# Attention's first steps beside the last feed-forward batch: another order, and key products copied out of PSUM

## The chip, the cores and the metric

The kernel runs on one core of one Trainium2 chip. The metric is the device time of one execution in microseconds; of several runs the median is taken. The core's engines are TensorE (PE, matrix products; its weight loads are shown as PEld), VectorE (DVE), ScalarE (ACT) and GpSimd (POOL), each with its own queue of instructions, and SyncE (SP), which here only issues DMA transfers. All data is float32.

## The reference

One "macaron" layer on x of shape (4, 512, 512): half a feed-forward block, an attention with a gated delta rule, and half a feed-forward block again, each behind a layer norm and added to its input.

```python
x = x + 0.5 * ffn(layernorm(x), gate_cp, up_cp, down_cp)
x = x + attn(layernorm(x), W_qkvz, W_ba, conv_w, dt_bias, A_log, norm_w, W_out)
x = x + 0.5 * ffn(layernorm(x), gate_cp, up_cp, down_cp)

# ffn: the three 2048 x 512 weights are cubic splines through control points
inter = silu(h @ gate_w.T) * (h @ up_w.T)
return inter @ down_w.T

# attn: 16 key heads, 32 value heads, 128 wide
q, k, v, z = split(x @ W_qkvz);  b_gate, a_gate = split(x @ W_ba)
q, k, v = silu(causal_conv4(q, k, v))
q, k = rms_norm(q) / 128, rms_norm(k) / 128**0.5
beta = sigmoid(b_gate);  g = -exp(A_log) * softplus(a_gate + dt_bias)
for t in range(512):                    # per batch and value head
    S = S * exp(g[t])
    S = S + outer(k[t], (v[t] - k[t] @ S) * beta[t])
    o[t] = q[t] @ S
return (silu(z) * rms_norm(o) * norm_w) @ W_out
```

The kernel does the recurrence in chunks of 128 tokens. In a chunk a lower triangular matrix of key products, weighted by decay and beta, has to be inverted; its 32 x 32 diagonal blocks are inverted first, for four heads at once.

## The kernel before, in words

**Three parts.** `ffn` is called for the first block, `attention` is a generator of steps, and `ffn` is called again. The first `ffn` is handed attention's generator as `beside`: while its last batch runs, each of its own steps is followed by one `next` on the generator (function `run`), and after the last of them the generator is run until it yields `None`. What is left is run after `ffn` has returned.

**The last feed-forward batch.** In the passage at hand `run` is called three times: with what is left of batch 2 (16 steps, together with the 16 gathers of batch 3's hidden rows, which POOL issues as indirect DMAs at L458), with batch 3's own steps (first four returns of batch 2: transposes at L509 and the additions on DVE at L537; then 32 steps of L482, L492, L495 and L498), and with batch 3's four returns. The hidden rows are stored by SP at L449, and a gather needs all of them.

**Order.** PE, DVE, ACT and POOL run this passage in the order in which the program emits it. SP is not in that hand-written order: a planner places its DMA issues. A calendar (`later`) puts follow-up work a number of ticks behind a step: a projection's taps one tick later, its tanh three after that, its silu one more.

**Attention's first steps** (`begin`, L1632 to the `yield None`). For batch 0: load constants; load four tiles of 128 rows of `x1` (two buffers, so tiles 2 and 3 follow tiles 0 and 1); statistics, one power on POOL and one normalisation for each tile (L920 to L927); four transposes `turn_x` (L934); the gate products `raw` (L941) with `gates_of` and `log1p`; then eight keys, one in seven ticks. `sums` (L1001 to L1016) makes the decays and stores them to DRAM. A key is: its weights loaded (L1080, one buffer), a projection in four steps (L1030), taps on ACT and DVE (L1038, L1040), tanh and silu (L1048, L1052), products of the key with itself in 32-wide blocks (`blocks`, L1061, into the tile `pkk`), their diagonal sums (L1066 to L1069), a power on POOL (L1071), weights (L1109 to L1119), and `below`: a scan over the decay row `ad` (L1126) and the product `dd` of `pkk` with its result (L1129). `invert` (L1140 to L1159) works on the `dd` of four keys; here two of its steps are put behind each tick.

**Banks.** Until the feed-forward block has given its PSUM back, attention has two banks, each with one buffer: `bank` hands out "kk" for `pkk`, and "bank" for all others (transposes, gate products, sums, projections). The banks of the main loop (`at_pa` and others) are opened when these two are closed.

**The main loop** takes one head in each of 66 slots (64 heads of four batches), each with its queries, values, gates, recurrence, output and, eight heads ahead, another key. In that loop keys have buffers of their own (`pa` is not `None`).

Of the kernel before, what the change touches and what calls it, by code (L numbers as in the profile page):

```python
# [11 lines left out]
F32 = mybir.dt.float32  # L12
BF16 = mybir.dt.bfloat16
AF = mybir.ActivationFunctionType
ALU = mybir.AluOpType
# [249 lines left out]
def tile_macaron(ctx, tc, x, w_qkvz, w_ba, conv_w, dt_bias, a_log, norm_w, w_out, cps, consts, grid, starts, out):  # L265
# [33 lines left out]
    def ffn(src, dst, build, beside=iter(())):  # L299
        with ExitStack() as st:  # L300
# [339 lines left out]
            with by_hand():  # L640
                also = beside if B > 2 else iter(())
                run(*left, also)
                run(*turn_of(B - 1), also)
                run(plan["tail"], [], also)
                drain()
                for step in beside:
                    if step is None:
                        break
# [167 lines left out]
    def attention():  # L816


        with ExitStack() as st:
# [14 lines left out]
            sm = pool("at_sm", 2)  # L834
            sn = pool("at_sn", LEAD + 3)
            w1 = split("at_w1", 1, "za", "ge", "w_k", "dd", "inv", "inv_tmp", "rn", "rt")
            w2 = split("at_w2", 2, "sq", "xnT", "acc", "th", "ad", "wed")
            wkeys = pool("at_k", LEAD + 2)
            first_banks = ExitStack()
            pf = first_banks.enter_context(tc.tile_pool(name="at_pf", bufs=1, space=PSUM))  # L840
# [2 lines left out]
            def bank(p, name, shape):  # L843
                if p is None:
                    return pf.tile(shape, F32, name=name, tag="kk" if name == "pkk" else "bank")
                return p.tile(shape, F32, name=name, tag="bank")


            cst = ac.tile([P, C_ID], F32, name="cst")
            nc.sync.dma_start(cst, consts[:, :C_ID])  # L850
            ones = ac.tile([P, P], F32, name="ones")
            nc.vector.memset(ones, 1.0)
            gt = cst[:, C_GT : C_GT + P]
            le = cst[:, C_LE : C_LE + P]
            idb = cst[:, C_IDB : C_IDB + BLK]

            cw = ac.tile([P, 4 * NK, 4], F32, name="cw")
            nc.sync.dma_start(cw, conv_w.rearrange("(n p) k -> p n k", p=P))
            nc.vector.tensor_scalar(cw, cw, 0.5, None, ALU.mult)
            wba = ac.tile([P, NC, 4 * NK], F32, name="wba")  # L860
            nc.sync.dma_start(wba, w_ba.rearrange("(c p) n -> p c n", p=P))
            dtb = ac.tile([P, NG], F32, name="dtb")
            nc.sync.dma_start(dtb, dt_bias.partition_broadcast(P))
            nega = ac.tile([P, NG], F32, name="nega")
            nc.sync.dma_start(nega, a_log.partition_broadcast(P))
            nc.scalar.activation(nega, nega, AF.Exp)
            nc.vector.tensor_scalar(nega, nega, -1.0, None, ALU.mult)
            nwh = ac.tile([P, 1], F32, name="nwh")
            nc.sync.dma_start(nwh, norm_w.rearrange("(p o) -> p o", o=1))
            nc.vector.tensor_scalar(nwh, nwh, 0.5, None, ALU.mult)  # L870

# [24 lines left out]

            tts = [ac.tile([P, 8, P], F32, name=f"tt{k}", tag=f"tt{k}") for k in range(2)]
            nn = ac.tile([64, 8, 64], F32, name="nn")  # L900
            for x_ in (*tts, nn):
                nc.vector.memset(x_, 0.0)

            decay_c, decay_b = (
                [dram.tile([NK, NT, 2, P], F32, name=f"decay_{k}{b}", tag=f"decay_{k}{b}") for b in range(B)] for k in "cb"
# [2 lines left out]
            def begin(b):  # L908


                bt, box = {}, {}

                def load(t):
                    xt = w2.tile([P, H], F32, name="xt", tag="sq")
# [141 lines left out]
            def products(out, v):  # L1056

                for t in range(NT):
                    for o in range(0, P, BLK):
                        blk = v[:, t * P + o : t * P + o + BLK]  # L1060
                        nc.tensor.matmul(out[o : o + BLK, t, :], blk, blk, start=True, stop=True)  # L1061
# [12 lines left out]
            def keys(b, n, bt, s, dd, slot):  # L1074

                at = n * 6 * DK + DK

                def load():
                    s["w_k"] = w1.tile([P, NC, DK], F32, name="w_k")
                    nc.sync.dma_start(s["w_k"], w_qkvz[:, at : at + DK].rearrange("(c p) k -> p c k", p=P))  # L1080

                def dest():
                    s["k"] = wkeys.tile([P, S], F32, name="k")
                    return s["k"]

                dense = project(lambda: s["w_k"], 0, NK + n, dest, bt)

                def decay():
                    s["ad"] = w2.tile([P, NT, 2, BLK], F32, name="ad")
                    for o in range(0, P, BLK):  # L1090
                        src = decay_b[b][n].rearrange("t r q -> (t r) q")[:, o : o + BLK]
                        nc.sync.dma_start(
                            s["ad"][o : o + BLK].rearrange("p t r q -> p (t r) q"), src.partition_broadcast(BLK)
                        )

                def blocks():
                    pkk = bank(pa, "pkk", [P, NT, BLK])
                    s["pkk"] = pkk
                    products(pkk, s["k"])

                    def squares():
                        ms, rs = mean_square(pkk, "k")
                        later(3, lambda: weights(ms, rs))

                    later(1, squares)

                def weights(ms, rs):
                    irk = sn.tile([P, NT], F32, name="irk")
                    nc.vector.scalar_tensor_tensor(irk, ms, DK**0.5, rs, ALU.mult, ALU.mult)  # L1109
# [12 lines left out]

                def below():
                    wed = s["wed"]
                    flat = wed.rearrange("p t r q -> p (t r q)")
                    nc.vector.tensor_tensor_scan(  # L1126
                        flat, s["ad"].rearrange("p t r q -> p (t r q)"), flat, 0.0, ALU.mult, ALU.add
                    )
                    nc.vector.tensor_tensor(  # L1129
                        dd()[:, 8 * slot : 8 * slot + 8, :].rearrange("p (t r) q -> p t r q", r=2),  # L1130
                        bc(s["pkk"], 2, 2), s["wed"], ALU.mult,
                    )

                return dict(load=load, dense=dense, decay=decay, blocks=blocks)
# [494 lines left out]
                    due()  # L1629
                    yield True  # L1630

            batches[0], load, turn_x, raw, sums = begin(0)  # L1632
            load(0)
            load(1)
            yield from ticks(9)
            turn_x(0)
            load(2)
            yield from ticks(2)
            turn_x(1)
            load(3)  # L1640
            yield from ticks(8)
            turn_x(2)
            yield from ticks(2)
            turn_x(3)
            yield from ticks(1)
            raw()
            yield from ticks(1)
            ahead = min(LEAD, N)
            made, first = [], None
            for un in range(ahead + 2):  # L1650

                if un < ahead:
                    made.append(keys_of(un))
                    made[un]["load"]()
                if un >= 2:
                    made[un - 2]["blocks"]()
                for i in range(7):
                    if un < ahead and i < NC:
                        made[un]["dense"][i]()
                    if un == 1 and i == 4:  # L1660
                        sums()
                    if 1 <= un <= ahead and i == 5:
                        made[un - 1]["decay"]()
                    yield from ticks(1)
                    for _ in range(2):
                        next(first or iter(()), None)
                if un == GRP + 1:
                    first = invert(diag[0], inverse[0])
            drain()
            for _ in first:  # L1670
                pass
            yield None
            first_banks.close()
            for f in backs:
# [49 lines left out]
```

## Time and profile before

| | us |
|---|---|
| median of 3 runs | 3895.45 (3895.11 to 3900.36) |
| the profiled execution | 3850.33 |
| its span, first to last instruction | 3848.6 |
| PE busy in it | 3584.5 (93%) |
| DVE busy | 2633.1 (68%) |
| ACT busy | 1461.8 (38%) |
| POOL busy | 851.7 (22%) |
| passage: last batch's leftovers begin on PE | 341.2 |
| first transpose of attention | 361.5 |
| first key's projection begins | 394.5 |
| last return of the feed-forward block on PE | 449.5 |
| first query projection of the main loop begins | 519.65 |
| first query products (`pqq`, L1061) begin | 530.56 |

A busy share is a mean over stages with different limits, so it says little of a passage of 180 us. Read the passage by stretches: which engine is idle, and which event ended its wait. An engine name with a q behind it (SPq) is that engine's queue. In lines of time the columns are start, duration, engine, source line, operation, tiles written and read, how many instructions were merged, and in brackets the idle time before with what ended it. In lines of waits they are the sum, the number and the longest.

### The profile page before, as it was taken

Reading aid. Unit: us, or ns where it says so; the run is one execution under the profiler, and the core shown is the slowest. Engines: PE = TensorE matmul, PEld = TensorE weight load, DVE = VectorE, ACT = ScalarE, POOL = GpSimd, SP = SyncE. Lnnn points to the kernel's source line nnn. Section 1 sums busy time; section 2 is a strip of 40 time slices with the busy share of each in tenths; the row PEclk is TensorE's granted clock in tenths of the full one; section 3 lists DMA queues with packets and bytes.
Section 4 is the critical chain, followed back from the end, with each engine's and each line's share of the span. In section 5 each row is a group of like instructions: output and inputs, shape, how many; then the busy total and the mean of one; then the engine's idle time right before and its main releaser. Section 6 shows DMA issues by size and latency. Waiting matters only on the chain.

```text
span 3848.6 us, 62481 instructions
## 1 busy us (share of the span) xinstructions
PE 3584.5 (93%) x24568; PEld 1970.3 (51%) x24568; DVE 2633.1 (68%) x5931; ACT 1461.8 (38%) x3432; POOL 851.7 (22%) x658
## 2 busy tenths in 40 slices
PE   5997768999999999999999999999999999997998
PEld 2332335555555555555555555555555555553333
DVE  5232577877888888787788887887888777652321
ACT  2221124444444444444444444444444444442221
POOL 2113112212222222122222221222222222120221
PEclk8999889999999999999999999999999999997999
DMA  4435311122212222122122221221122211112452
GB/s 142 154 131 177 102 46 50 58 66 63 59 59 59 61 86 76 43 66 72 60 58 86 61 69 55 61 61 58 58 81 68 67 50 56 50 36 97 152 200 91
DMA packets 303093, 302.25 MB, mean 79 GB/s; under 512 B 96880, under 2 KB 231312, under 8 KB 302224
## 3 DMA queue, kind: packets, MB, share of 16 engines
q1 hardware_dynamic: 292560, 264.70, 22.0%
q0 software_dynamic: 10240, 33.56, 2.8%
q8 instruction: 194, 3.18, 0.3%
q14 instruction: 99, 0.81, 0.1%
HBM read 247.60 MB, written 50.59 MB: 77 GB/s over the span
## 4 chain that ended last, share of the span: by engine, by line
PE 43%; DVE 36%; ACT 8%; POOL 6%; issue 3%; DMA 3%; SPq 1%; DVEq 0%; POOLq 0%; ACTq 0%
DVE acc L1040 13%; PE py L1492 7%; PE pz L1344 6%; DVE vT L1052 4%; PE pj L1030 4%; PE y L492 3%; POOL oo L1465 3%; DVE ee L1212 3%; PE pg L439 3%; PE pu L439 3%; PE pks L1383 2%; POOL orr L1464 2%; ACT tq L1400 2%; PE pu L1329 2%; ACT th L1048 2%
## 5 line engine op out<-in xcount | busy, mean ns | idle before, releaser
L1040 DVE SCALAR_TENSOR_TENSOR acc<-pj,cw,acc 128x511 f32<-128x511 f32 (+2 forms) x768 | 573.7, 747 | 166.1 <-ACT acc L1038 148.0
L1030 PE MATMUL pj<-xnT,w_v 128*128 128x512 f32 x1024 | 519.4, 600 | 0.0
L1492 PE MATMUL py<-w_o,gT 128*128 128x512 f32 x1024 | 514.9, 616 | 0.4
L1344 PE MATMUL pz<-w_z,xnT 128*128 128x512 f32 x1024 | 514.1, 613 | 0.0
L448 DVE TENSOR_TENSOR ffn_it<-pu,ffn_sg 128x512 f32<-128x512 f32 x128 | 88.4, 691 | 365.8 <-PE pu L439 252.5
L1030 PE MATMUL pj<-xnT,w_q 128*128 128x512 f32 x512 | 255.8, 603 | 4.9 <-DVE dd L1129 4.9
L1030 PE MATMUL pj<-xnT,w_k 128*128 128x512 f32 x512 | 260.1, 612 | 0.0
L1038 ACT ACTIVATE acc<-pj,cw 128x512 f32<-128x512 f32 x256 | 175.1, 684 | 212.9 <-PE pj L1030 212.0
L1400 ACT ACTIVATE tq<-pks,rqe 128x128 f32<-128x128 f32 x384 | 120.0, 364 | 340.0 <-DVE rq L1241 204.9
L1048 ACT ACTIVATE th<-acc 128x512 f32<-128x512 f32 x256 | 163.0, 637 | 214.9 <-DVE acc L1040 213.2
L1470 ACT ACTIVATE oo<-oo,orr 128x128 f32<-128x128 f32 x512 | 162.6, 389 | 204.4 <-POOL oo L1465 204.4
L1492 PEld LDWEIGHTS py<-w_o,gT 128*128 128x128 f32 x1024 | 171.5, 192 | 106.2 <-issue 95.2
L1344 PEld LDWEIGHTS pz<-w_z,xnT 128*128 128x128 f32 x1024 | 169.9, 191 | 99.4 <-issue 88.4
L1071 POOL TENSOR_TENSOR rsq<-msq,phalf 128x4 f32<-128x4 f32 x64 | 64.8, 1013 | 684.9 <-DVE msq L1069 684.9
L1071 POOL TENSOR_TENSOR rsk<-msk,phalf 128x4 f32<-128x4 f32 x64 | 65.9, 1029 | 658.9 <-DVE msk L1069 649.2
L1030 PEld LDWEIGHTS pj<-xnT,w_v 128*128 128x128 f32 x1024 | 170.2, 191 | 70.1 <-issue 63.5
L1226 POOL TENSOR_TENSOR ks<-kn,ws 128x1024 f32<-128x1024 f32 x64 | 121.6, 1901 | 375.7 <-DVE ws L1219 352.3
L1052 DVE SCALAR_TENSOR_TENSOR vT<-th,acc 128x512 f32<-128x512 f32 x128 | 185.1, 1446 | 22.8 <-ACT th L1048 22.8
L458 POOL DMA_INDIRECT nat<-hid,idx x128 | 122.2, 955 | 305.1 <-PE y_pt L509 104.2
L1458 DVE TENSOR_REDUCE om<-osq 128x4 f32<-128x512 f32 x128 | 87.1, 681 | 138.8 <-ACT osq L1457 138.8
L1151 DVE TENSOR_TENSOR inv<-inv,inv_tmp 128x30 f32<-128x30 f32 (+14 forms) x480 | 168.4, 351 | 16.5
L1408 PEld LDWEIGHTS pzz<-rr,tt 128*128 128x128 f32 x768 | 114.6, 192 | 113.0 <-issue 54.7
(205 smaller groups left out, 6868.3 us busy)
## 6 DMA issues: line engine op xcount, KB each, us to landing
hid<-ffn_it SPq DMA_DIRECT2D x128, 256.0 KB, 2.0
w_v<-in_L_attn_W_qkvz SPq DMA_DIRECT2D x64, 512.0 KB, 3.6
w_z<-in_L_attn_W_qkvz SPq DMA_DIRECT2D x64, 512.0 KB, 5.1
ab<-decay_c SPq DMA_DIRECT2D x64, 512.0 KB, 3.7
w_o<-in_L_attn_W_out SPq DMA_DIRECT2D x32, 1024.0 KB, 5.5
w_k<-in_L_attn_W_qkvz SPq DMA_DIRECT2D x64, 256.0 KB, 2.8
w_q<-in_L_attn_W_qkvz SPq DMA_DIRECT2D x64, 256.0 KB, 3.3
ad<-decay_b SPq DMA_DIRECT2D x256, 32.0 KB, 2.2
```

The source lines that it names most:

```text
L439: nc.tensor.matmul(pm, wc[k // 2][:, m, at : at + P], ft[k // 2], start=True, stop=True)
L1030: nc.tensor.matmul(pj, w()[:, c, col : col + DK], xnT[:, c, :], start=c == 0, stop=c == NC - 1)
L1038: nc.scalar.activation(acc, pj, AF.Copy, scale=cw[:, ch, 3:4])
L1040: nc.vector.scalar_tensor_tensor(acc[:, d:], pj[:, : S - d], cw[:, ch, 3 - d : 4 - d], acc[:, d:], ALU.mult, ALU.add)
L1048: nc.scalar.activation(th, box["acc"], AF.Tanh)
L1052: nc.vector.scalar_tensor_tensor(dest(), box["th"], 1.0, box["acc"], ALU.add, ALU.mult)
L1071: nc.gpsimd.tensor_tensor(rs, ms, phalf[:, :NT], ALU.pow)
L1151: nc.vector.tensor_tensor(ee[:, j + 1 :, :j], ee[:, j + 1 :, :j], tj, ALU.add)
L1344: nc.tensor.matmul(pz, xnT[:, c, t * P : (t + 1) * P], pair["wz"][:, c].rearrange("p j k -> p (j k)"), start=c == 0, stop=c == NC - 1,)
L1400: nc.scalar.activation(tq[:, r], pks[:, 1, r], AF.Copy, scale=s["rqe"][:, t, r : r + 1])
L1470: nc.scalar.activation(s["oo"][:, t, r], s["oo"][:, t, r], AF.Copy, scale=s["orr"][:, u : u + 1])
L1492: nc.tensor.matmul(box["py"], pair["gT"][r][:, t, :], pair["wo"][:, r, :], start=r == 0, stop=r == 3)
```

## The change

The feed-forward side: the last batch's first four steps (batch 2's returns) are run as before; then the generator is pulled 14 times with no step between; then the other 32 steps.

The attention side: (1) the four row tiles are loaded at the very head, into four buffers (`sq` and `acc` tags), ahead of the constants. (2) The arithmetic on the constants moves into `constants()`, called after the transposes; the memsets of `tts` and `nn` move behind the last key. (3) One bias addition and one power serve all four tiles. (4) The first key's projection comes before `raw`, which is called at step 5 of key 0; `sums` at step 5 of the third turn; the products of a key come at step 6 of the turn two later, and with them the load of its decays. (5) While the keys run with the two early banks, `pkk` is copied to an SBUF tile `ksq` by ACT, and what follows reads the copy. The loop has 11 turns instead of 10, and `invert` begins at step 6 of turn 6.

```diff
-                run(*turn_of(B - 1), also)
+                units, _ = turn_of(B - 1)
+                run(units[:NT], [], also)
+                for _ in range(14):
+                    next(also, None)
+                run(units[NT:], [], also)
...
+            xts = []
+            for t in range(NT):
+                xts.append(w2.tile([P, H], F32, name="xt", tag="sq" if t < 2 else "acc"))
+                nc.sync.dma_start(xts[t], x1[0][t * P : (t + 1) * P, :])
...
+            def constants():
+                nc.vector.tensor_scalar(cw, cw, 0.5, None, ALU.mult)
+                nc.scalar.activation(nega, nega, AF.Exp)
+                nc.vector.tensor_scalar(nega, nega, -1.0, None, ALU.mult)
+                nc.vector.tensor_scalar(nwh, nwh, 0.5, None, ALU.mult)
+                nc.vector.memset(ones, 1.0)
...
                     pkk = bank(pa, "pkk", [P, NT, BLK])
+                    products(pkk, s["k"])
+                    if pa is None:
+                        ksq = w2.tile([P, NT, BLK], F32, name="ksq")
+                        nc.scalar.copy(ksq, pkk)
+                        pkk = ksq
                     s["pkk"] = pkk
-                    products(pkk, s["k"])
...
-            load(0)
-            load(1)
-            yield from ticks(9)
-            turn_x(0)
-            load(2)
-            yield from ticks(2)
-            turn_x(1)
-            load(3)
-            yield from ticks(8)
-            turn_x(2)
-            yield from ticks(2)
-            turn_x(3)
-            yield from ticks(1)
-            raw()
-            yield from ticks(1)
+            yield from ticks(1)
+            mv = sm.tile([P, NT, 2], F32, name="fr_mv")
+            for t in range(NT):
+                st_ = sm.tile([P, 6], F32, name="at_st")
+                nc.vector.bn_stats(st_, xts[t])
+                nc.vector.bn_aggr(mv[:, t, :], st_)
+            var = sm.tile([P, NT], F32, name="fr_var")
+            nc.vector.tensor_scalar(var, mv[:, :, 1], LN_EPS, None, ALU.add)
+            rstd = sm.tile([P, NT], F32, name="fr_rstd")
+            nc.gpsimd.tensor_tensor(rstd, var, phalf[:, :NT], ALU.pow)
+            for t in range(NT):
+                nc.vector.tensor_scalar(
+                    xts[t], xts[t], mv[:, t, 0:1], rstd[:, t : t + 1], ALU.subtract, ALU.mult
+                )
+                batches[0]["box"][t] = xts[t]
             yield from ticks(8)
+            for t in range(NT):
+                turn_x(t)
+                yield from ticks(1)
+            constants()
...
-            for un in range(ahead + 2):
+            for un in range(ahead + 3):
                 if un < ahead:
                     made.append(keys_of(un))
                     made[un]["load"]()
-                if un >= 2:
-                    made[un - 2]["blocks"]()
                 for i in range(7):
                     if un < ahead and i < NC:
                         made[un]["dense"][i]()
-                    if un == 1 and i == 4:
+                    if un == 0 and i == 5:
+                        raw()
+                    if un == 2 and i == 5:
                         sums()
-                    if 1 <= un <= ahead and i == 5:
-                        made[un - 1]["decay"]()
+                    if 2 <= un < ahead + 2:
+                        if i == 6:
+                            made[un - 2]["decay"]()
+                            made[un - 2]["blocks"]()
+                    if un == GRP + 2 and i == 6:
+                        first = invert(diag[0], inverse[0])
                     yield from ticks(1)
                     for _ in range(2):
                         next(first or iter(()), None)
-                if un == GRP + 1:
-                    first = invert(diag[0], inverse[0])
             drain()
             for _ in first:
                 pass
+            for x_ in (*tts, nn):
+                nc.vector.memset(x_, 0.0)
```

More of the change, by code (lines that the diff above doesn't have):

```diff
@@ L836, in attention @@
             w1 = split("at_w1", 1, "za", "ge", "w_k", "dd", "inv", "inv_tmp", "rn", "rt")
-            w2 = split("at_w2", 2, "sq", "xnT", "acc", "th", "ad", "wed")
+            w2 = split("at_w2", 2, "sq", "xnT", "acc", "th", "ad", "wed", "ksq")
             wkeys = pool("at_k", LEAD + 2)
@@ L851, in attention @@
             ones = ac.tile([P, P], F32, name="ones")
-            nc.vector.memset(ones, 1.0)
             gt = cst[:, C_GT : C_GT + P]
@@ L858, in attention @@
             nc.sync.dma_start(cw, conv_w.rearrange("(n p) k -> p n k", p=P))
-            nc.vector.tensor_scalar(cw, cw, 0.5, None, ALU.mult)
             wba = ac.tile([P, NC, 4 * NK], F32, name="wba")
@@ L865, in attention @@
             nc.sync.dma_start(nega, a_log.partition_broadcast(P))
-            nc.scalar.activation(nega, nega, AF.Exp)
-            nc.vector.tensor_scalar(nega, nega, -1.0, None, ALU.mult)
             nwh = ac.tile([P, 1], F32, name="nwh")
             nc.sync.dma_start(nwh, norm_w.rearrange("(p o) -> p o", o=1))
-            nc.vector.tensor_scalar(nwh, nwh, 0.5, None, ALU.mult)
+            def constants():
[4 more added lines that the diff above has]
+                nc.vector.memset(ones, 1.0)
             clock, calendar = [0], {}
@@ L900, in attention @@
             nn = ac.tile([64, 8, 64], F32, name="nn")
-            for x_ in (*tts, nn):
-                nc.vector.memset(x_, 0.0)
             decay_c, decay_b = (
@@ L911, in begin @@
                 bt, box = {}, {}
+                bt["box"] = box
                 def load(t):
@@ L1630, in ticks @@
                     yield True
-            batches[0], load, turn_x, raw, sums = begin(0)
-            load(0)
-            load(1)
-            yield from ticks(9)
-            turn_x(0)
-            load(2)
-            yield from ticks(2)
-            turn_x(1)
-            load(3)
-            yield from ticks(8)
-            turn_x(2)
-            yield from ticks(2)
-            turn_x(3)
-            yield from ticks(1)
-            raw()
-            yield from ticks(1)
+            batches[0], _, turn_x, raw, sums = begin(0)
+            yield from ticks(1)
[13 more added lines that the diff above has]
+                batches[0]["box"][t] = xts[t]
+            yield from ticks(8)
+            for t in range(NT):
+                turn_x(t)
+                yield from ticks(1)
+            constants()
             ahead = min(LEAD, N)
             made, first = [], None
-            for un in range(ahead + 2):
+            for un in range(ahead + 3):
                 if un < ahead:
```

## The prediction

> **What bounds the kernel now.** I read the page first, then the busy time of each engine by stretch, then the waits of the stretch in which the edited lines run (341 to 520 us), then the chain of waits there, and at last the instructions in order of time. Over the whole run TensorE (PE) carries the time; the slices say where it does not:
>
> ```profile
> PE   5997768999999999999999999999999999997998
> PEclk8999889999999999999999999999999999997999
> ```
>
> A slice is 96.2 us. The fourth to sixth digits of PE (7, 7, 6: 289 to 577 us) hold the passage from the first feed-forward block (FFN) to attention, the weakest place after the start. By stretch (length, then busy us of PE, weight load, DVE, ACT, POOL, then granted clock):
>
> ```profile
> 350.30:361.50 11.20, 0.00 (x0) 0.02 (x1) 4.83 (x12) 1.51 (x2) 4.04 (x5) 0.68 0.32 119
> 374.90:394.50 19.60, 17.38 (x70) 9.68 (x69) 7.90 (x51) 2.56 (x6) 3.48 (x4) 0.59 0.34 108
> 394.50:450.00 55.50, 51.12 (x316) 20.34 (x312) 26.46 (x73) 9.69 (x18) 6.35 (x8) 0.99 0.17 39
> 450.00:519.60 69.60, 21.13 (x186) 9.61 (x184) 54.37 (x160) 5.01 (x8) 8.74 (x11) 0.65 0.35 106
> 560.00:1500.00 940.00, 905.78 (x6747) 537.09 (x6746) 756.27 (x1653) 405.67 (x985) 218.26 (x146) 0.99 0.22 64
> ```
>
> The main loop (last line) has PE at 96%, so what the passage saves comes off the end one for one. PE loses 11.2 us at 350.3 and 48 of the 69.6 us after 450. The waits give both reasons:
>
> ```profile
> PE pkk L1061 <- DVE dd L1129: 45.3, 7, 11.1
> PE ln_pt L934 <- DVE xt L927: 14.5, 2, 11.2
> DVE nega L867 <- ACT nega L866: 6.5, 1, 6.5
> ACT L866 <- DMA nega<-in_L_attn_A_log: 13.4, 1, 13.4
> ```
>
> After 450 the FFN has no more work to give, and each of five remaining keys goes through a ring; one turn of it in the chain:
>
> ```profile
> 472.37 0.66 PE pkk L1061 x32
> 473.02 5.76 PE pj L1030 x8
> 478.80 0.70 ACT acc L1038
> 479.52 0.76 DVE acc L1040
> ...
> 484.63 0.70 DVE wed L1126
> 485.35 0.42 DVE dd L1129
> ```
>
> The single bank of key products is released only when DVE has made `dd` of it; PE stands before the next products with the next key's projection queued behind. At 350.3 PE stands before the first transpose, and the rest of the FFN's totals queue behind that:
>
> ```profile
> 342.25 5.34 SPq L449 DMA_DIRECT2D hid<-ffn_it  x1
> 349.11 0.29 DVE L859 TENSOR_SCALAR cw<-cw 128x256 f32<-128x256 f32 x1 [6.87 <-DMA cw<-in_L_attn_conv_w]
> 349.72 16.44 SPq L915 DMA_DIRECT2D xt<-x  x4
> 358.77 0.63 DVE L920 BATCH_NORM_STATS2 at_st<-xt 128x6 f32<-128x512 f32 x1
> ```
>
> The rows are asked for at 349.7, behind the constants, and their statistics stand on DVE behind the constants' arithmetic and 2.3 us of memsets.
>
> **The Trainium skill.** (1) TensorE: Matmul & The Clock Gate, "Step-by-step: what each phase is for": only weight loads are pulled ahead, matmuls stay in program order. The trace agrees: nothing of L498 passes the stalled L934. (2) The same page, "What's actually happening": an idle array falls to half clock after about 3.4 us and needs as long a busy stretch to recover. The trace agrees: the eight matmul records of a key's projection take 5.76 to 6.25 us after 450 at a granted 0.59 to 0.64, while two of them take 0.86 us beside the FFN at 0.99, so 3.44 for a key. (3) DMA: Bandwidth & Descriptors, "Why small descriptors are slow": each descriptor pays a fixed overhead. `cw` is 128 x 64 pieces of 16 bytes; it lands after 7.4 us, `cst`, of about its bytes, after 3.6, and the hidden-state store behind it holds SP 5.34 us, where such a store usually takes 0.32.
>
> **The change part by part.** Attention's first steps are a generator, pulled once per FFN step. Before it yields 93 times: 16 beside the third batch's leftovers, 36 and 4 beside the last batch, 37 alone. After, it yields 90 times: 16, 4 (the returns), 14 pulled alone, 32 and 4, and 20 alone. Key u begins at pull 14 + 7u, against 24 + 7u.
>
> *Rows first.* SP reaches the rows at 341.3 instead of 349.7. The planner orders SP, so I can't know what passes what; I take two rows, the last hidden store, two rows, then constants. The rows then land by about 347 (their median landing is 4.4 us), four statistics cost 4 x 0.85 = 3.4 us of DVE, one power on POOL about 0.9 (rows of 0.6 to 1.0), so the first normalised row is at about 350.3. PE arrives at the transpose at 350.3 with ten FFN units done. The 11.2 us stall is all but gone, and with it a POOL stop of 6.2 us between gathers. If the store is behind `cw` as now, the power, queued on POOL behind two gathers, comes at 352.6, and 3.5 us are lost. Three powers fewer save nothing more: they lay beside gathers.
>
> *Constants later.* `cw`, `nega` and `nwh` are wanted first by the taps of key 0; their DMAs land by 357 and ACT's table load (1.28 us) is beside FFN units. The `tt` and `nn` memsets (0.91 + 0.91 + 0.48 = 2.3 us) go to the end of DVE's queue, where they cost in full.
>
> *First key before the gates, and 14 pulls alone.* After four transposes (1.46 us a pull with a total, from 350.4) key 0 is projected among the last totals: done 362.3. Its taps end at 365.5 and free the one shared bank; the gate products follow (3.68 us warm in a later batch, 7.02 here at 0.59): 369 to 372.6. From their end R: gate arithmetic frees the bank at R + 0.9; key 1 (3.44) R + 4.4; its taps stand on DVE behind the gates' logarithm (5.6 us) and leftover returns (1.6): R + 11.4; key 2 and taps R + 18.3 to 21; sums and transposes R + 23.7; products of key 0 R + 24.2. With R = 370.6 the FFN's `sums(0)` starts at 394.8. At 394.5 today four of these units are done and no key; then three keys, sums and the first products are done, and no unit. The stretch is bank-bound, not PE-bound: this is the price of the 14 pulls.
>
> *The overlapped stretch.* From there 32 units, 4 returns and keys 3 to 7 remain. Today 28 units, 4 returns, five keys and the sums took 394.5 to 450. Four more units cost 4.2 us, two more sets of products 1.0, the sums' 4.2 go: 56.5 us, to 451. All eight keys are then projected, warm, where today only five are.
>
> *Products copied.* The copy is 128 x 128 from PSUM on ACT; the nearest row, `beta`, takes 0.28 us, and ScalarE: Activation LUTs, "What ACT_TABLE_LOAD costs", prices it at 186 ns + 0.833 x 128 = 0.29 us (an estimate). Eight of them, 2.3 us, on an engine busy 5 of 69.6 us. In exchange PE never waits for `dd`; `dd` itself reads SBUF, which I price at nothing. The 45.3 us wait goes.
>
> *What is late next: DVE.* The inversion of the first four keys starts at pull 62, about 439. From there DVE holds: inversion 9.90 + 9.97 + three transposes 5.7, with gaps 27.1; returns 6.4; two silus 1.4; taps 2.3; weights, `dd` and squares of keys 4 to 7, 2.65 + 4.4 + 2.25; the scan at L1212 2.3; memsets 2.3. Sum 51.1. To this come waits that have no cover at the end: POOL's power and `wed` for the last two keys, 3 us, and 2 for the `ab` row, which DVE waited 2.09 for today. 439 + 51 + 5 = 495. PE has meanwhile run into the main loop as far as its banks go and stands before the q products; those need DVE's next inversion transpose 1.9, taps 2.3, ACT 0.65, silu 0.7: 500.6. Today they start at 530.56. Gain 30 us.
>
> **Sum.** 3850.33 for the profiled execution becomes about 3820. The runs shown have a median of 3895.45, 45 us above that one execution; I take the same 30 us off: 3865. The stretch's unknowns (R by 3 us either way, the warm clock of keys 1 and 2, row order 3.5, DVE's waits 0 to 8) give 3853 to 3878.
>
> **Rivals.**
> - *The bank-bound stretch is longer* (chance 0.2). Cold PE, or a key's weights asked for late: the order on SP puts `w_k` of key 3 behind the decay stores, which wait for each other. That costs up to 12 us and moves all behind it: gain 15, 3880. For it: that stretch ran at 0.59. Against: today w_k of key 2 goes out before the sums' stores.
> - *DVE is less of a wall* (0.13): it keeps pace beside the FFN and ends at 483 instead of 495: gain 42, 3853. For it: it was busy only 26.5 of 55.5 us there. Against: the inversion cannot start before key 3's `dd`.
> - *The copy frees nothing* (0.07): keys stay tied to DVE's order so that the saving stays within 0.2% (7.8 us, what this measurement tells from no change): 3890. Against: five of eight keys no longer pass that place alone.
> - *Slower* (0.10): the main loop's SP order, which the planner makes anew with other buffers, puts a weight load behind a waiting decay load in every slot. Its price is the stall times 64 slots; above 30 / 64 = 0.47 us a slot it eats the gain; at 1 us, 3929. For it: L1092 already waits 36 us for DVE in the passage. Against: the loop's code is the same.
>
> The forecast itself has 0.5. **Range** 3848 to 3887: it leaves out the slower case and most of "frees nothing". Faster by over 0.2%: 0.5 + 0.2 + 0.13, same 0.07, slower 0.10.
>
> **What would show it.** First transpose within 2 us of 350; gate products ending near 370; FFN sums starting near 395 and the FFN's last PE work near 451; no wait of PE for `dd`, and the eighth key's projection before 455; DVE busy almost without gap from 439 to the main loop; q products near 500. I am wrong if FFN sums start after 405, if DVE has gaps of over 10 us after 451, or if slots of the main loop change length.

## The result, and the profile after

The changed kernel takes 3872.02 us (median of four runs, 3868.04 to 3876.63). The kernel before, timed beside it, takes 3895.28 us (3895.09 to 3900.36). The ratio is 0.9938 with a 95% interval of 0.992 to 0.9955. The gain is 23.3 us, and the interval allows 17.5 to 31.2.

The two profiled executions cannot be compared by their spans. The one after took 3876.63 us, close to its timed runs. The one before took 3850.33 us, 45 us less than its own timed runs. The page and the waits of after show where such time comes from. First the page's slices (96.9 us each):

```profile
PE   5988779999999999999999999999999999988798
PEclk8999889999999999999999999999999999989998
```

The fourth to seventh digits were 7, 7, 6, 8 and are now 8, 7, 7, 9. The third digit, in the first FFN, fell from 9 to 8, and digits near the end fell too. The change touches neither place. The waits of ACT over the whole run of after (engine, line, what it waited for: us in total, times, longest):

```profile
ACT fm L484 <- remote: 26.3, 3, 13.6
...
ACT ft L378 <- remote: 24.0, 4, 7.2
...
ACT ffn_xnT L369 <- remote: 20.5, 2, 11.0
```

One of these stops in the instructions of after in order of time (start, length, engine, line, and in brackets the idle time before it and what ended it):

```profile
232.91 0.96 POOL L458 DMA_INDIRECT nat<-hid,idx  x1 [0.30 <-issue]
234.18 0.96 POOL L458 DMA_INDIRECT nat<-hid,idx  x1 [0.30 <-issue]
234.80 0.59 ACT L369 COPY ffn_xnT<-ln_pt 128x512 f32<-128x512 f32 x1 [10.97 <-remote]
...
235.44 3.40 PE L374 MATMUL pf<-ffn_xnT,lag 128*32 128x512 f32 x16 [10.43 <-issue]
```

ACT stands 11 us and PE stands behind it, while POOL issues gathers; `remote` means that the profile names no instruction that ended the wait. The profile of before has no wait of this kind. Cutting both runs at the same instructions places the difference:

| stretch | before, us | after, us | difference |
|---|---|---|---|
| start to the passage (first L492 product of the leftovers) | 341.24 | 359.87 | +18.6 |
| passage to the first q products (L1072 on `q`) | 189.32 | 159.52 | −29.8 |
| from there to the q products of the fourth slot | 129.19 | 132.49 | +3.3 |
| from there to those of the last slot | 2765.62 | 2766.77 | +1.1 |
| from there to the last `py` | 84.97 | 84.99 | 0.0 |
| last FFN, after the last `py` | 338.26 | 371.16 | +32.9 |

The first and last rows are the stops. The changed lines run in the second row. From here on the text and its tables count times from the passage's first product, so that the stops in the FFN stay out; lines of the profile keep their own count from the span's start.

Busy time by stretch in after (stretch, length, then busy us and instructions of PE, weight load, DVE, ACT, POOL, then granted clock, DMA share, GB/s):

```profile
359.87:370.47 10.60, 9.06 (x43) 3.76 (x43) 5.04 (x12) 0.00 (x0) 3.59 (x4) 1.00 0.79 182
410.50:466.50 56.00, 55.29 (x424) 20.70 (x418) 29.55 (x90) 11.45 (x23) 10.29 (x13) 0.98 0.26 64
458.95:515.60 56.65, 19.10 (x143) 9.33 (x141) 51.02 (x152) 4.56 (x9) 8.42 (x9) 0.69 0.42 128
```

The first line runs from the passage's start to the first transpose, where the 11.2 us stop was; PE now stands only 1.54 us in it. The second is the FFN with keys, PE at 99%. The third runs from the inversion's first instruction to the first taps of the main loop. In it the roles have changed: PE is busy 19 of 56.65 us and DVE 51. An engine whose own work fills a stretch like this is called its wall below. The waits of after in the passage say the same:

```profile
ACT ksq L1112 <- DVE dd L1144: 24.7, 2, 22.1
...
PE pkk L1072 <- DVE k L1063: 19.2, 1, 19.2
...
PE pqq L1072 <- DVE q L1063: 12.7, 1, 12.7
...
PE pj L1041 <- ACT ksq L1112: 9.4, 1, 9.4
```

PE no longer waits for `dd` itself (45.3 us before). It waits for DVE at other places instead, and in the last of these lines for `dd` by way of ACT's copy. The instructions of after at the two ends of the passage:

```profile
361.13 2.58 SPq L856 DMA_DIRECT2D xt<-x  x3
...
364.70 8.38 SPq L869 DMA_DIRECT2D wba<-in_L_attn_W_ba  x1
...
368.59 1.04 POOL L1657 TENSOR_TENSOR fr_rstd<-fr_var,phalf 128x4 f32<-128x4 f32 x1 [0.91 <-DVE fr_var L1655]
...
370.47 0.63 PE L945 MATMUL ln_pt<-ident,xt 128*128 128x128 f32 x4 [1.54 <-DVE xt L1659]
...
384.82 6.67 PE L952 MATMUL pb<-wba,xnT 128*128 128x64 f32 x32 [2.30 <-issue]
...
495.88 0.27 ACT L1112 COPY ksq<-pkk 128x128 f32<-128x128 f32 x1 [22.06 <-DVE dd L1144]
496.19 6.22 PE L1041 MATMUL pj<-xnT,w_q 128*128 128x512 f32 x8 [9.44 <-ACT ksq L1112]
...
515.62 2.27 DVE L1051 SCALAR_TENSOR_TENSOR acc<-pj,cw,acc 128x511 f32<-128x511 f32 x3
...
519.39 0.66 PE L1072 MATMUL pqq<-q 128*32 128x32 f32 x32 [12.69 <-DVE q L1063]
```

The wait before the first transpose is 1.54 us instead of 11.2. At the other end the eighth key's copy stands 22.06 us, because its buffer, one of two, is held until `dd` of the sixth key has read it. The q projection queues behind that. It still comes 13 us before DVE takes up its result (496.19 + 6.22 against 515.62), so this new wait costs nothing here.

### The profile page after: what moved, and what is told of

The parts are those of the page before. It is cut to its first block, busy times and chain, and to the rows that moved or that the text cites. A ratio compares the mean times of both kernels' runs of the same rounds, so it can differ in the third digit from the quotient of the medians.

```text
span 3874.8 us, 62477 instructions
## 1 busy us (share of the span) xinstructions
PE 3587.5 (93%) x24568; PEld 1969.3 (51%) x24568; DVE 2633.2 (68%) x5928; ACT 1464.5 (38%) x3440; POOL 852.4 (22%) x655
## 4 chain that ended last, share of the span: by engine, by line
PE 44%; DVE 36%; ACT 8%; POOL 5%; issue 3%; another core or an unknown queue 1%; DMA 1%; SPq 0%; DVEq 0%; ACTq 0%; POOLq 0%
DVE acc L1051 12%; PE py L1507 7%; PE pz L1359 6%; DVE vT L1063 4%; PE pj L1041 4%; PE pg L439 3%; PE pu L439 3%; PE y L492 3%; POOL oo L1480 3%; DVE ee L1227 3%; PE pks L1398 2%; POOL orr L1479 2%; ACT tq L1415 2%; PE pu L1344 2%; ACT oo L1485 2%
```

## The experiments

Twelve runs followed, the two kernels again and ten others. Each was read from one profile, by these marks: the start of the first transpose on PE, the start of the gate products, the first FFN product of the last batch's own steps (L482, "FFN sums"), the end of the last FFN work on PE, the inversion's first instruction on DVE, and the first query products of the first and of the fourth slot of the main loop. None of the twelve profiles has one of the stops, and all their times lie near 3850 us or below, with the kernel before at 3845 to 3857 us beside them. The kernel before itself put the fourth slot's q products at 318.51 us in one profile and 321.28 in another, so a passage difference below about 3 us is not told apart. "Before" in a difference is the profile with 318.51; against the other one each gain would be 2.8 us larger.

| kernel | first transpose | gates | FFN sums | last FFN PE work | inversion | first q products | fourth slot's | one time (before beside it) |
|---|---|---|---|---|---|---|---|---|
| before | 20.27 | 44.36 | 33.63 | 108.90 | 132.56 | 189.32 | 318.51 | 3850.33 |
| e0_before | 20.02 | 44.05 | 33.36 | 113.00 | 135.46 | 192.09 | 321.28 | 3852.70 (3852.50) |
| after | 10.60 | 24.95 | 50.64 | 106.62 | 99.08 | 159.52 | 292.01 | 3876.63 |
| e8_after | 10.39 | 24.79 | 50.99 | 106.69 | 99.15 | 159.51 | 290.68 | 3822.70 (3847.44) |
| e1_no_copy | 10.53 | 25.10 | 49.16 | 118.44 | 102.04 | 166.13 | 295.53 | 3830.26 (3852.50) |
| e2_copy_alone | 19.81 | 43.88 | 33.19 | 110.86 | 129.37 | 179.23 | 310.56 | 3841.10 (3852.50) |
| e3_rows_alone | 10.53 | 24.79 | 18.86 | 90.55 | 112.98 | 169.43 | 298.44 | 3829.50 (3852.50) |
| e4_no_pulls | 10.93 | 25.29 | 32.00 | 91.60 | 112.89 | 163.29 | 294.48 | 3827.92 (3847.44) |
| e9_rows_copy | 11.30 | 25.59 | 19.63 | 86.60 | 107.16 | 157.02 | 288.26 | 3818.59 (3847.44) |
| e6_memset_early | 10.73 | 26.37 | 52.06 | 108.02 | 100.47 | 158.42 | 290.41 | 3822.97 (3847.44) |
| e10_pulls28 | 10.90 | 25.26 | 64.68 | 114.71 | 91.91 | 151.22 | 280.33 | 3811.71 (3850.60) |
| e10_pulls34 | 10.71 | 25.06 | 72.59 | 122.15 | 92.34 | 151.67 | 281.36 | 3813.81 (3850.60) |
| e11_rows_copy_pulls28 | 10.72 | 21.13 | 61.63 | 126.49 | 97.29 | 157.33 | 287.08 | 3818.31 (3850.60) |
| e12_best | 10.37 | 24.71 | 62.60 | 112.62 | 89.82 | 149.09 | 278.17 | 3803.12 (3848.35, medians) |

**The two kernels again.** The kernel before, unchanged:

> The kernel before, unchanged, profiled once more. The shown profile of before is 45 us shorter than its timed runs; the profile of the changed kernel has, in both feed-forward blocks, engines that stand for 5 to 11 us while the gathers are issued, some 18 us in the first and 33 us in the last, and the shown profile of before has none. Theory A (such stops belong to single executions of either kernel): this profile shows them too, with a time near 3880 to 3900, and the passage from the leftovers' first product to the fourth slot's q products is again 318.5 us within 0.5. Theory B (the change brings the stops): no stop, a time near 3850.

and the changed kernel, unchanged:

> The changed kernel, unchanged, profiled once more beside a kernel before that takes some 3852 us here. If the stops in the feed-forward blocks belong to where and when a kernel ran and not to the change: none here, passage to the fourth slot's q products 292 us within 1, last feed-forward block near 339 us instead of 371, time 3824 to 3828. If the change brings them: they are here again, and the time is above 3860.

The kernel before lay at 3852.70 us without a stop, which by itself spoke for theory B, and its passage missed the expected 318.5 us by 2.8. The changed kernel then lay at 3822.70 with before at 3847.44 beside it, a gain of 24.7 us, and it has no stop either. Its last FFN takes 340.46 us, where the profile of after had 371.16. So the stops are not something that the change always brings, and the gain is there without them.

**The change without the copy.**

```diff
-                    if pa is None:
-                        ksq = w2.tile([P, NT, BLK], F32, name="ksq")
-                        nc.scalar.copy(ksq, pkk)
-                        pkk = ksq
```

> The changed kernel without the copy to ksq. Theory 1 (after the reordering DVE is the wall from the inversion on, and dd of a key is already emitted before the next products): the passage to the fourth slot's q products goes from 292.0 to 293 to 296 us, though PE waits for dd again. Theory 2 (the copy, which removes a wait of 45 us, carries the gain): 305 us or more.

The waits of PE in the passage of this kernel:

```profile
PE pkk L1072 <- DVE dd L1140: 43.9, 7, 20.6
```

The wait of 45 us is back in nearly its full size, and the fourth slot comes only 4.9 us later than in e8_after (295.53 against 290.68), as theory 1 expected. DVE is the wall in both: from the inversion to the taps it is busy 51.05 of 60.27 us here and 50.97 of 56.60 in e8_after. So the wait costs 3.6 us of gaps in DVE's work there, and the inversion starts 2.9 us later. A sum of waits on PE is no measure of what removing them gives.

**The copy alone, in the kernel before.**

```diff
+            w2 = split("at_w2", 2, "sq", "xnT", "acc", "th", "ad", "wed", "ksq")
...
+                    products(pkk, s["k"])
+                    if pa is None:
+                        ksq = w2.tile([P, NT, BLK], F32, name="ksq")
+                        nc.scalar.copy(ksq, pkk)
+                        pkk = ksq
                     s["pkk"] = pkk
-                    products(pkk, s["k"])
```

> The kernel before with the copy alone. Theory 1 (in the old order three keys are left for the time after the feed-forward block, and DVE has 54 us of work there): 8 to 11 us off the 318.5 us of the passage. Theory 2 (the ring of products and dd is the bound): 20 us or more off.

The fourth slot's q products came at 310.56, 8.0 us before those of before: theory 1, at its lower end.

**The rows first and one power, alone.** The order of keys and gates is that of before. The memsets of `tt` and `nn` stand behind the constants' arithmetic, and both stand behind the transposes. These parts ("the rows" below) were not tried one by one.

```diff
+            xts = []
+            for t in range(NT):
+                xts.append(w2.tile([P, H], F32, name="xt", tag="sq" if t < 2 else "acc"))
+                nc.sync.dma_start(xts[t], x1[0][t * P : (t + 1) * P, :])
...
+            nc.gpsimd.tensor_tensor(rstd, var, phalf[:, :NT], ALU.pow)
...
+            constants()
+            for x_ in (*tts, nn):
+                nc.vector.memset(x_, 0.0)
```

> The kernel before with rows first, one power, and the arithmetic on constants and the memsets behind the four transposes; order of gates and keys, banks and pulls as before. Theory 1 (the 11.2 us stop of PE goes through to the end because everything behind it is in a chain): 8 to 12 us off the 318.5 us. Rival (later waits for the gathered rows or for DVE take the gain back): 0 to 3 us off.

This missed: 298.44 is 20.1 us before the kernel before, nearly double what was expected. The instructions of e3_rows_alone show how the stretch begins:

```profile
350.59 0.63 PE L940 MATMUL ln_pt<-ident,xt 128*128 128x128 f32 x4 [1.47 <-DVE xt L1650]
...
364.86 3.79 PE L947 MATMUL pb<-wba,xnT 128*128 128x64 f32 x32
```

and its stretches, from the FFN sums to the FFN's last work on PE and from there to the first q products:

```profile
358.90:430.60 71.70, 65.14 (x381) 26.81 (x380) 35.21 (x121) 13.98 (x26) 13.10 (x16) 0.95 0.30 84
430.60:509.50 78.90, 31.00 (x205) 13.65 (x204) 59.25 (x166) 6.99 (x13) 8.74 (x11) 0.65 0.32 95
```

The first transpose is 9.7 us earlier than before, the gate products start 19.6 earlier, the FFN's last PE work is 18.4 earlier, and the fourth slot 20.1. So the stop itself is only half of what the rows are worth. The rest arises between the first transpose and the gates. This stretch in before, with one of its waits, and then in e3_rows_alone:

```profile
361.51:385.60 24.09, 18.55 (x69) 8.63 (x69) 10.12 (x53) 5.17 (x9) 13.84 (x16) 0.78 0.60 181
374.31 0.63 PE L934 MATMUL ln_pt<-ident,xt 128*128 128x128 f32 x4 [3.31 <-DVE xt L927]
...
350.59:364.85 14.26, 13.87 (x68) 6.95 (x68) 7.92 (x48) 6.56 (x11) 10.91 (x12) 1.00 0.88 224
```

PE does the same work in both. Before, it stood 5.5 us in the stretch, most of it for the third row tile, and was busy 18.55 us at a granted clock of 0.78; now it stands 0.4 us and is busy 13.87 us at 1.00. So of the 9.8 us that are saved here, 5.2 are waits and 4.7 are the slower clock. The gate products that follow take 3.79 us at 1.00, where they took 7.09 at 0.50 before. The Trainium skill (TensorE: Matmul & The Clock Gate, "What's actually happening") says that an idle array runs at half clock until it has been busy for a while; the two durations agree with half and full clock. How long that while is doesn't agree: the page puts it at about 3.4 us, but before stayed at 0.50 from 384 to 394 us, with PE at work all ten of them.

**The change without the 14 pulls.**

```diff
-                for _ in range(14):
-                    next(also, None)
```

> The changed kernel without the 14 pulls made alone. Theory 1 (DVE is the wall from the inversion on; without the pulls the inversion begins after the feed-forward block has ended and its key runs on a cold PE): passage 295 to 298 us instead of 292.0. Rival (the pulls only leave PE idle for 24 us that feed-forward units could fill): 280 to 288 us.

The fourth slot's products came at 294.48, 3.8 us after those of e8_after: just short of what was expected of a real gain from the pulls, and little more than the spread between two profiles. The FFN is done 15.1 us earlier without the pulls and the inversion starts 13.7 us later, and the two nearly cancel.

**Rows and copy, in the old order, without pulls.** The edits of e2_copy_alone and e3_rows_alone together:

> Rows first as in the run of rows alone, and the copy, in the old order of gates and keys and without the pulls. If the parts add up: 318.5 - 20.1 - 8.0 = 290.4 us, no worse than the whole change with its 292.0, so that the new order brings nothing. If the new order is needed for the copy to pay (theory 1 as predicted: keys must be finished beside the feed-forward block): 295 us or more.

The fourth slot's products came at 288.26. The two parts together do what the whole change does (290.68), and a little better by 2.4 us, which is within the spread. The stretches of e9_rows_copy, cut as for e3_rows_alone:

```profile
359.30:426.30 67.00, 62.52 (x388) 26.11 (x390) 34.25 (x114) 14.69 (x29) 13.13 (x16) 1.00 0.31 88
426.30:496.70 70.40, 28.71 (x203) 12.40 (x202) 60.02 (x172) 7.83 (x17) 8.75 (x11) 0.73 0.37 107
```

In the first PE is at 93% and never leaves full clock. In the second DVE has 60.02 of 70.40 us of work, against 59.25 of 78.90 in e3_rows_alone: the copy takes no work from DVE, it takes out gaps.

**The memsets earlier.**

```diff
+            for x_ in (*tts, nn):
+                nc.vector.memset(x_, 0.0)
             ahead = min(LEAD, N)
...
             for _ in first:
                 pass
-            for x_ in (*tts, nn):
-                nc.vector.memset(x_, 0.0)
```

> The changed kernel with the memsets of tts and nn straight after the arithmetic on the constants instead of behind the last key. If DVE is the wall up to the main loop, the first q products come 2.3 us earlier, at 157.2 us from the leftovers' first product instead of 159.5, and the fourth slot's follow by about as much (290). If PE or SP is the wall: no change within 0.5 us.

From the inversion to the q products DVE's wall is 57.95 us long instead of 60.36 in e8_after: 2.4 us shorter, the 2.3 us of the memsets. But the gates come 1.6 us later and the inversion 1.3, and of the gain 1.1 us is left at the first q products and 0.3 at the fourth slot. The wall is DVE, but its work is not free ahead of the gates either.

**More pulls.** If the inversion starts earlier, more of DVE's wall lies beside the FFN.

```diff
-                for _ in range(14):
+                for _ in range(28):
```

> The changed kernel with 28 pulls made alone instead of 14, so that two more keys run before the feed-forward units and the inversion begins beside them. If DVE's work from the inversion on is the wall (60 us from there to the first q products, whatever PE does): inversion at about 90 us instead of 99, first q products at 149 to 153 instead of 159.5, the fourth slot's at 281 to 285 instead of 290.7. If PE's idle time in the pulls made alone counts: the feed-forward work ends later than DVE's, and the fourth slot is at 290 or later.

> The changed kernel with 34 pulls alone, the most that the 90 yields allow. DVE as the wall: inversion at 85 to 88 us, first q products at 145 to 151. PE as the bound: the feed-forward block's last product, which came at 106.7 with 14 pulls, is at 135 or later and the main loop begins behind it, no better than with 28.

With 28 pulls the inversion starts at 91.91, the first q products are at 151.22 and the fourth slot at 280.33, 10.3 us before e8_after. With 34 (the same line, `range(34)`) nothing more comes: the inversion does not start earlier (92.34), and the FFN ends 7.4 us later. Both expectations for 34 missed their marks, the inversion at 85 to 88 us as well as the FFN's end at 135 or later, though it is no better than with 28, as the second had said.

The same 28 pulls in the old order, with rows and copy (e9_rows_copy with the diff's split of `turn_of`):

> Rows first and the copy in the old order of gates and keys (157.0 us to the first q products, 288.3 to the fourth slot's), with 28 pulls alone added at the same place. DVE as the wall: the inversion begins at about 90 us instead of 107, first q products at 146 to 152, as good as the new order with 28 pulls, which shows that the order of gates and first key is worth nothing. If the new order is worth something once the pulls are there: 155 or more.

The fourth slot's products came at 287.08, 1.2 us from e9_rows_copy without pulls. The new order without pulls, e4_no_pulls, is 6.2 us behind e9_rows_copy. So the pulls alone give about nothing and the order alone costs; together, in e10_pulls28, they are worth 7.9 us over e9_rows_copy. ("Order" takes in the place of the memsets, which e6_memset_early puts at 0.3 us.) Why the pulls pay only in the new order was not tried.

**The version that beats both.** 28 pulls, and the last memsets on POOL:

```diff
-                for _ in range(14):
+                for _ in range(28):
...
-                nc.vector.memset(x_, 0.0)
+                nc.gpsimd.memset(x_, 0.0)
```

> The changed kernel with 28 pulls alone and the three memsets on POOL instead of DVE, at the same place in the program. If DVE is the wall up to the main loop, taking 2.3 us of its work away brings the first q products from 151.2 to 148.9 us and the fourth slot's from 280.3 to 278; POOL has time for them. If PE is held elsewhere (it stands 25 us for its first projection of the main loop): no change within 0.5 us. Against the kernel before: a ratio of 0.989 to 0.990, about 41 us less; the change itself stands at 0.9938.

It takes 3803.12 us (median of four, 3801.86 to 3804.55) against 3848.35 of before (seven runs, 3844.89 to 3856.89): 0.9878, interval 0.986 to 0.9897, a gain of 45.2 us. Both marks came almost where the expectation had put them, 149.09 and 278.17, but by luck. The memsets' part did not show: from inversion to q products it is 59.27 us here and 59.31 in e10_pulls28. What came earlier by 2.1 us is the inversion, and the gate products took 3.76 us here against 6.08 there, though the two kernels are the same up to them. The instructions of e12_best, and behind them the last taps line of e10_pulls28, tell why the memsets no longer count:

```profile
474.12 3.05 DVE L537 TENSOR_TENSOR ffn_xr<-y_pt,ffn_xr 128x4 f32<-128x4 f32 x26
...
477.43 6.48 PE L1041 MATMUL pj<-xnT,w_q 128*128 128x512 f32 x8 [25.36 <-DVE rk L1126]
...
484.71 2.32 DVE L1051 SCALAR_TENSOR_TENSOR acc<-pj,cw,acc 128x511 f32<-128x511 f32 x3 [3.09 <-ACT acc L1049]
...
487.71 2.31 DVE L1051 SCALAR_TENSOR_TENSOR acc<-pj,cw,acc 128x511 f32<-128x511 f32 x3 [0.68 <-ACT acc L1049]
```

PE stands 25.4 us before the q projection, then runs it in 6.48 us, and DVE stands 3.09 us for its result, where it stood 0.68 with the memsets among its own work: the time that they left free became a wait. The projection starts just after the last returns of the FFN end on DVE (474.12 + 3.05); the profile names the next instruction but one, `rk`. That fits a bank of the main loop that lies over a bank of those returns, but this was inferred from the times and not tried.

Two things were not tried: a third buffer for the copied products, and the constants' DMAs ahead of the rows with all else changed. The cause of the stops also stays open.

## Why the prediction was right, and where it was not

The forecast of 3865 us was 7 us below the result. The direction was right, and so was the course of the passage, mark by mark. How the gain divides among the parts of the change was not. The marks, less the prediction's own 341.2 us for the passage's start:

| step | predicted | measured in after |
|---|---|---|
| first transpose | 9.2 | 10.60 |
| gate products end (R) | 29.4 | 31.6 |
| FFN sums | 53.6 | 50.64 |
| FFN's last PE work | 109.8 | 106.62 |
| inversion | 97.8 | 99.08 |
| end of DVE's wall, before the next inversion's transpose | 153.8 | 154.06 |
| first main-loop taps on DVE, after that transpose | 155.7 | 155.75 |
| first q products | 159.4 | 159.52 |

- *Rows first.* The SP order I assumed held except that the last hidden store went behind one row and not two. The first transpose came 1.4 us late. Right for this mark.
- *First key before the gates, and 14 pulls.* R was 2.2 us late, mostly because the gate products took 6.67 us, near the cold end (7.02) of the two durations between which I had put R; in e8_after, the same kernel, they took 5.86. From R to the sums it was 19.0 us where I had summed 24.2: keys 1 and 2 were the over-sized term (their taps end at R + 16.0, not R + 21). The rival of a longer bank-bound stretch is refuted.
- *The overlapped stretch* was 55.98 us against 56.5.
- *Products copied.* A copy takes 0.27 us against the estimated 0.29. "PE never waits for `dd`" held. That "the 45.3 us wait goes" did not make the gain: e1_no_copy puts 43.9 us of it back for 4.9 us.
- *DVE as the wall.* From the inversion to the next inversion's transpose I summed 51.1 us, 1.5 of them gaps within the inversion, and 5 of waits: 56. It ran 54.98 us, with DVE busy 49.35. e6_memset_early confirms it: 2.3 us less in it made the way to the q products 2.4 shorter. The rival in which DVE is less of a wall is refuted.
- *"PE has meanwhile run into the main loop as far as its banks go"* was wrong. The two `ksq` buffers tie the eighth copy to DVE, and the q projection starts at 136.32, 9.4 us after the last key's products. It cost nothing, as DVE decided.
- *"What the passage saves comes off the end one for one"* is the step that failed in the sum. The passage gave 29.8 us as forecast (30), but the first slot grew from 38.53 to 41.27 us and the second from 44.68 to 45.25, and 26.5 was left at the fourth slot. In e8_after the first slot is 39.98, and in e10_pulls28 it is 38.53 again. The longer first slot (39.98 to 41.27) stands in the six profiles where the q projection is done long before DVE takes it up; in the other eight, where the taps follow it at once, it is 38.53. So the mark of the first q products flatters the change by about 1.5 to 2.7 us. I had named changed slots as a sign of error, without a price.
- *The slower rival* (a stall in every slot from a new order on SP) fell: from the fourth to the last slot the loop took 1.1 us more in after and 0.6 less in e8_after than before, where that rival needs 30. The rival in which the copy frees nothing fell with the gain as a whole, 17.5 us at least by the interval; of the copy itself 4.9 to 8.0 us are shown.
- What remains between 26.5 and the timed 23.3 lies inside the interval, and with stops in the FFN, whose size differs between executions, I don't split it further.

What the marks hid is where the gain came from. I booked the rows as an 11 us stop and treated the new order as the rest's vehicle. The experiments give the rows alone 20.1 us, the copy alone 8.0, and both together 30.3 (318.51 − 288.26), all that the change gives. The reordering with 14 pulls adds nothing beyond them (−2.4 us, within the spread). So the total was right partly by luck: one part, sized too small, stood in for another without worth.

## What to carry to other kernels

When an engine's stop is removed early in a chain, look at what ran cold or late behind it: here a stop of 11 us was worth 20. Once another engine is the wall, a long wait on the first can be a mere symptom; sum the wall's own work from its first input, and move that input forward, as 28 pulls with the new order did for 10 us. Where profiled executions differ in places that the change doesn't touch, cut both at the same instructions before reading any difference.

## What the runs showed of the hardware that was not expected

- ACT stood up to 13.6 us at a time, and DVE up to 9.9, in lines of the FFN in one execution, the waits ended by nothing that the profile shows. In the profile of after this is 18.6 + 32.9 us against before. The kernel before has been timed at 3895 us on one occasion and at 3845 to 3857 on others; that its slower runs have the same stops is inferred, since its profile is of 3850 us.
- The same 32 gate products took 3.76 to 7.09 us. In the three profiles with the rows late they took 7.09 each time, in before at a granted 0.50. In e3_rows_alone, where nothing stops PE ahead of them, they took 3.79, and the eight us around them were granted 1.00 with PE at work 7.63. In after PE stands 2.30 us before them, and they took 6.67, at 0.58 with PE at work 7.18 of eight us. But the stop does not fix the price: e8_after is the same kernel and took 5.86, and e12_best, the same up to here and with the same stop of 2.30 us, took 3.76 at 1.00. What decides between these was not found.
- In after, SP stands 8.38 us in the issue of `wba`, right behind `cw` with its 16-byte pieces; behind the same transfer the hidden store stood 5.34 us before. The next issue of the queue stands behind `cw` in all fourteen profiles: 5.3 to 5.7 us in the three with the old order of loads, 7.5 to 8.9 in the others. The Trainium skill (DMA: Bandwidth & Descriptors, "Why small descriptors are slow") gives each descriptor a fixed cost. That the number of pieces is what holds the queue fits this, but no run changed it.
